# Two rounds of a relational layer and one of a graph convolution summed transposed, with degrees and decoded counts prepared earlier

## The chip, the cores and the metric

The kernel runs on one core of a Trainium2 chip. The metric is the device time of one execution in microseconds. Three executions of the kernel before gave 1709.08, 1710.58 and 1712.69 us; the median is 1710.58 us.

The profile names the engines PE (TensorE, the matrix multiplier; PEld is its loading of the stationary operand), DVE (VectorE), ACT (ScalarE), POOL (GpSimd) and SP (SyncE, which here only issues DMAs). Each works through its own list of instructions in order and waits for the others by semaphores. In a matmul one operand stands still (at most 128 x 128, "stationary") and the other is streamed past it ("moving"); the result lands in PSUM, with the columns of the stationary operand across its partitions and the columns of the moving one along them.

## The reference

Four blocks of a graph network work on 512 nodes with 768 features in float32, over one list of 8704 edges. Each ends with a residual and a layer normalization:

```python
x = _layernorm(x + gat(x))     # layer 0: 8 heads, two rounds
x = _layernorm(x + rgat(x))    # layer 1: 3 edge types, two rounds (r1, r2)
x = _layernorm(x + rgcn(x))    # layer 2: 4 edge types, three rounds (c1, c2, c3)
x = _layernorm(x + gcn(x))     # layer 3: two rounds (d1, d2)
```

The change touches the last two. One round of layer 2 is

```python
out = x @ root + bias
for r in range(4):
    h_r = x @ weight[r]
    # mean over the edges of type r that come into a node
    out = out + segment_sum(h_r[src] * norm[r][:, None], dst)    # norm = 1 / max(degree_r[dst], 1)
```

with a relu behind c1 and c2. One round of layer 3 is `segment_sum((x @ W)[src] * dinv[src] * dinv[dst], dst) + b`, with self loops, where dinv is 1/sqrt of a node's degree, and a relu behind d1.

## The kernel before, in words

**Edges as counts.** The edge list is turned once into matrices of counts: how many edges of a type lead from node s to node t. Seven counts (three types of layer 1, four of layer 2) are packed as digits into one integer; packed_store and packedT_store in DRAM hold that matrix and its transpose. `digit` and `digit_sum` take out a digit or a sum of digits. A sum over edges is then a product with a 512 x 512 matrix cT. Its four tiles of 128 x 512, one per block k of source nodes, have the source nodes across the partitions and the target nodes along them.

**Products in three passes.** A product of 512 nodes x 768 with a weight half (768 x 384) keeps float32 accuracy in three passes[...]. The nodes lie transposed as S: three tiles hi, lo and df of 128 x 6 x 512, six chunks of 128 features across the partitions, 512 nodes along them. The weight half is cut the same way into hm, lo and df (`split_piece`: ACT L771, DVE L772 and L773, three pieces of 128 x 768 per half, loaded by SP at L759 at most three ahead). `product` runs over the four blocks of 128 nodes: six times L814 (hi with hm) and L817 (lo with lo), an ACT instruction that scales the sum in place (L820), and six times L825 (df with df). The six of L825 come behind the next group's twelve (`open_group`, `close_group`), so that PE doesn't wait for ACT. The piece of S (128 features x 128 nodes) is stationary, and the weights move, 384 wide. The result has nodes across and features along.

**A round of layer 2.** Two root products go into acc (`keep`, with the bias added on DVE). Then eight products follow, one for each type r and half j. Each result h is split into hi and lo by `split_h` (ACT L1669, DVE L1670), again with nodes across. After each product comes the aggregation of the one before it, `agg`: for each of four blocks of target nodes eight matmuls (L1682, L1686), with cT's 128 x 128 piece stationary and h moving, 384 wide. DVE multiplies the sum by 1/degree, a number per partition, and adds it to acc in one instruction (L1790).

**Between rounds.** acc has nodes across, but S needs features across. `split_nodes` transposes each block of 128 nodes on PE, two groups of six pieces in halves of three (L785), and cuts the result: hi on ACT with the relu (L790), lo and df on DVE (L792 or L794, L795). `last_two` lets that run between the last aggregations, and the end of block 3 runs inside the next round's first product (`late_end`). d1 passes to d2 in the same way; its aggregation is `agg` at L1841.

**Degrees and counts.** In c1 and half 0 the h tile carries two more columns of ones, so the matmuls of L1682 are 386 wide there, and the extra column of the sum is the degree: L1786 copies it, L1787 and L1788 make 1/degree. The cT tiles are decoded in c1 between the groups of a product: `digit` on DVE (L165), a cast on ACT (L1703). The sum of the digits plus the identity, for layer 3, is made with the last type (L1712). SP stores the tiles to cT_store, and c2, c3 and d1 fetch them from there by POOL's queue, 1 MB each (L1757).

**Before layer 2.** r2, the last round of layer 1, has its three types' products first (r_p), with the first softmax steps among them (L1448, L1451, L1453, L1457). Then `sum2` sums each of four node blocks over 12 pieces of softmax weights (soft_wT, transposed by PE at L1473), in two halves (r_o, L1621), normalizes the block (`norm`, L843 to L849) and hands it to `split_nodes` (x_t).

**Order.** The program is written in one order, and a scheduler orders each engine's instructions by estimated times and dependences, so that an instruction can stand far from where its line is. SP, POOL, ACT and DVE run what it gave them in that order.

Of the kernel before, what the change touches and what calls it, by code (L numbers as in the profile page):

```python
# [8 lines left out]
F32 = mybir.dt.float32  # L9
# [13 lines left out]
P = 128  # L23
# [11 lines left out]
def gnn_stack_kernel(ctx: ExitStack, tc: tile.TileContext, a: dict, out: bass.AP):  # L35
# [125 lines left out]
    flag = const.tile([1, 1], I32, tag="flag", name="flag")  # L161

# [546 lines left out]
    def split_layers():  # L709
# [93 lines left out]
        def product(left, evac, name, between=()):  # L803

            u = used[0]
            used[0] += 1
            while cut[0] < PIECES * (u + 1):
                split_piece()
            hm, lo, df = forms.pop(u)
            for b in range(NB):  # L810
                bs = slice(b * P, (b + 1) * P)
                po = bank(f"{name}_{b}")
                for k in range(KC):
                    nc.tensor.matmul(  # L814
                        po[:, :HD], left[0][:, k, bs], hm[:, k, :], start=(k == 0), stop=False
                    )
                    nc.tensor.matmul(  # L817
                        po[:, :HD], left[1][:, k, bs], lo[:, k, :], start=False, stop=(k == KC - 1)
                    )
                nc.scalar.mul(po[:, :HD], po[:, :HD], SPLIT + 1.0)  # L820
                close_group()

                def rest(b=b, bs=bs, po=po):
                    for k in range(KC):
                        nc.tensor.matmul(  # L825
                            po[:, :HD], left[2][:, k, bs], df[:, k, :],
                            start=False, stop=(k == KC - 1), skip_group_check=True,
                        )
                    evac(b, po)

                open_group.append(rest)
                for job in between[b : b + 1]:
                    job()
                split_piece()
# [92 lines left out]
        with (  # L927
# [107 lines left out]
            seen = g.tile([P, 2, NB], F32, tag="seen", name="seen")  # L1035
# [234 lines left out]

            def check_counts():
# [14 lines left out]
            for i in range(H0):  # L1286
# [7 lines left out]
                elif i + 1 < H0:  # L1294
# [7 lines left out]
                    elif i == 3:  # L1302
                        more = [lambda: None, check_counts]
# [55 lines left out]
        with (  # L1359
# [245 lines left out]

            def finish2(b):
# [4 lines left out]
            def sum2(b, wT):  # L1611
# [3 lines left out]
                for j in range(2):  # L1615
# [14 lines left out]
                    )  # L1630
                    if j == 0 and b:
                        finish2(b - 1)
# [28 lines left out]
        def new_h(name):  # L1661
            hi = work.tile([P, NB, HD + 2], F32R, tag="h_hi", name=f"{name}_hi")
# [3 lines left out]
        def split_h(h, b, po, scale=None):  # L1666
            hi, lo = (t[:, b, :HD] for t in h)
# [9 lines left out]
        def aggregate(cT, h, b, name, ones=0):  # L1677
# [3 lines left out]
            for k in range(NB):  # L1681
                nc.tensor.matmul(  # L1682
                    po[:, : HD + ones], cT[:, k, bs], h[0][:, k, : HD + ones],
                    start=(k == 0), stop=False,
                )
                nc.tensor.matmul(  # L1686
                    po[:, :HD], cT[:, k, bs], h[1][:, k, :], start=False, stop=(k == NB - 1)
                )
            return po

        packedT = tail.tile([P, NB, N], I32, tag="packedT", name="packedT_b")
        nc.sync.dma_start(packedT, packedT_store)
# [4 lines left out]
        def decode(cT, r, k):  # L1697

            v = packedT[:, k, :]
            if r < R4 - 1:  # L1700
                d = work.tile([P, N], I32, tag="dig", name=f"dig{r}_{k}")
                digit(d, v, R3 + r)
                nc.scalar.copy(cT[:, k, :], d)  # L1703
            else:
                sums = [
                    work.tile([P, N], I32, tag=f"dig{i}", name=f"sum{i}_{k}") for i in range(2)
                ]
                for i in range(2):
                    digit_sum(sums[i], v, 3 * i)
                nc.vector.tensor_sub(cT[:, k, :], sums[0], sums[1])  # L1710
                t = work.tile([P, N], F32R, tag="tot", name=f"tot{k}")
                nc.scalar.copy(t, sums[0])  # L1712
                diag = t[:, k * P : (k + 1) * P]
                nc.vector.tensor_add(diag, diag, ident)
                nc.sync.dma_start(cT_store[R4, :, k, :], t.bitcast(F32))
            if k == NB - 1:
                nc.sync.dma_start(cT_store[r], cT.bitcast(F32))

# [3 lines left out]
        deg = tail.tile([P, R4, NB], F32, tag="deg", name="deg")  # L1722
        rdeg = tail.tile([P, R4, NB], F32, tag="rdeg", name="rdeg")
        dinv = tail.tile([P, NB], F32, tag="dinv", name="dinv")

# [19 lines left out]
        late_end = None  # L1745


        for i in (1, 2, 3):
            name = f"c{i}"
            brow = bias_row(a[f"L2_gnn_b{i}"], f"{name}_b")  # L1750
            brows = {i: brow}
            cTs = {}

            def fetch(r):
                cTs[r] = new_c(f"{name}_cT{r}")
                if i > 1:
                    nc.gpsimd.dma_start(cTs[r], cT_store[r])  # L1757

            if i == 3:
                for b in range(NB - 1):  # L1760
                    residual(x_store[1, b], b, brow)
            for j in range(2):

                def keep(b, po, i=i, j=j, brow=brow):
                    half = acc[:, b, columns_of(j)]
                    other = half if i == 3 else brow[:, columns_of(j)]
                    nc.vector.tensor_add(half, po[:, :HD], other)

                jobs = ()
                if late_end:  # L1770

                    def job(late_end=late_end, i=i, brow=brow):
# [149 lines left out]
```

## Time and profile before

| what | us |
|---|---|
| median of three runs | 1710.58 |
| profiled execution | 1706.29 |
| its span, first to last instruction | 1704.70 |
| PE busy | 1619.9 (95%) |
| DVE busy | 1181.0 (69%) |
| ACT busy | 772.3 (45%) |
| POOL busy | 54.0 (3%) |

The granted clock of PE over the whole span is 0.976 of full speed. The stages that matter here, by the times at which they run in the profiled execution:

| stage | from | to |
|---|---|---|
| r2's last product and softmax steps | 994 | 1015 |
| r2's sums (r_o) | 1015 | 1082 |
| c1 | 1085 | 1262 |
| c2 | 1262 | 1438 |
| c3 | 1438 | 1618 |
| d1 | 1618 | 1661 |
| d2 | 1661 | 1704 |

All times below are counted from the start of the span. In a row of the profile the line and engine come first, then the operation, the tile written, the tiles read, and the shapes; "x6" is a number of instructions. In the order of time the first two columns are start and length in us, and "[2.88 <-DVE r_y L849]" is idle time of the engine just before, with what ended it. A PE matmul overlaps the next one, so its pace is the distance of starts, not its length.

### The profile page before, as it was taken

What the parts mean: (1) busy time and instruction counts of PE and PEld (TensorE: products, weight loads), DVE (VectorE), ACT (ScalarE), POOL (GpSimd) and SP (SyncE); (2) the same over time, 40 slices, a digit from 0 to 9 for tenths busy, and PEclk for the clock granted to TensorE, in tenths of its full rate; (3) what the DMA queues carried; (4) which work ended last, traced back from release to release, by engine and by line L of the source; (5) the groups of instructions that cost most, each with busy time, mean ns of one, the idle gap of its engine ahead of it and who ended that gap; (6) DMA issues with size and microseconds to landing.
All of it is one profiled execution on the core that took longest, in us unless ns stands there. A gap on an engine that the chain in (4) does not pass through costs nothing.

```text
span 1704.7 us, 22298 instructions
## 1 busy us (share of the span) xinstructions
PE 1619.9 (95%) x8571; PEld 1444.5 (85%) x8571; DVE 1181.0 (69%) x2185; ACT 772.3 (45%) x1340; POOL 54.0 (3%) x71
## 2 busy tenths in 40 slices
PE   5999999999999999998898899999999999999897
PEld 2868879697887958898898796799999999999897
DVE  8978889786978797545784773655766456654764
ACT  5755656454545544333873371333333333323242
POOL 0000000000000010000001000000000002000001
PEclk8999999999999999998899999999999999999999
DMA  3333323132322222321003241332333224332321
GB/s 122 98 94 103 97 84 124 56 101 76 119 67 83 66 93 75 94 66 56 33 25 134 70 139 37 142 93 81 112 99 107 83 89 143 102 90 81 114 64 54
DMA packets 81266, 151.93 MB, mean 89 GB/s; under 512 B 5768, under 2 KB 67584, under 8 KB 79360
## 3 DMA queue, kind: packets, MB, share of 16 engines
q1 hardware_dynamic: 76048, 125.96, 23.9%
q0 software_dynamic: 3600, 20.47, 3.6%
q10 hardware_dynamic: 1504, 4.00, 0.6%
q8 instruction: 69, 1.13, 0.3%
q14 instruction: 45, 0.37, 0.1%
HBM read 133.63 MB, written 16.78 MB: 88 GB/s over the span
## 4 chain that ended last, share of the span: by engine, by line
PE 81%; DVE 12%; ACT 4%; issue 1%; DMA 1%; ACTq 0%; DVEq 0%; SPq 0%
PE g_o L1117 10%; PE c_p L825 6%; PE c_p L817 6%; PE c_p L814 6%; PE c_a L1682 4%; PE c_a L1686 4%; PE r_o L1621 4%; PE g_p L814 3%; PE g_p L817 3%; PE g_s L817 3%; PE g_s L814 3%; PE g_p L825 3%; PE g_s L825 3%; PE r_p L814 3%; PE r_p L817 3%; PE r_p L825 2%
## 5 line engine op out<-in xcount | busy, mean ns | idle before, releaser
L772 DVE SCALAR_TENSOR_TENSOR w<-w,raw 128x768 fp32r<-128x768 f32 x234 | 221.6, 953 | 120.8 <-ACT w L771 120.0
L771 ACT ACTIVATE w<-raw 128x768 fp32r<-128x768 f32 x234 | 195.1, 839 | 121.0 <-PE c_p L814 34.3
L773 DVE TENSOR_TENSOR w<-w,w 128x768 fp32r<-128x768 f32 x234 | 219.1, 950 | 2.9 <-PE r_p L825 1.5
L817 PE MATMUL c_p<-w,s 128*128 128x384 f32 x576 | 192.5, 334 | 0.0
L814 PE MATMUL c_p<-w,s 128*128 128x384 f32 x576 | 192.5, 334 | 0.0
L1117 PE MATMUL g_o<-wT,g_h 128*128 128x512 f32 x384 | 166.8, 594 | 6.7 <-ACT wT L1073 6.7
L1117 PEld LDWEIGHTS g_o<-wT,g_h 128*128 128x128 f32 x384 | 72.3, 190 | 96.4 <-issue 86.8
L1670 DVE TENSOR_TENSOR c_h_lo<-c_p,c_h_hi 128x384 fp32r<-128x384 f32 x96 | 53.2, 554 | 129.9 <-ACT c_h_hi L1669 129.9
L814 PE MATMUL g_p<-w,s 128*128 128x384 f32 x384 | 134.7, 351 | 0.0
L820 ACT ACTIVATE c_p<-c_p 128x384 f32<-128x384 f32 x96 | 45.6, 475 | 192.9 <-PE c_p L817 192.5
L814 PE MATMUL g_s<-w,y 128*128 128x384 f32 x384 | 132.0, 344 | 0.0
L817 PE MATMUL g_s<-w,y 128*128 128x384 f32 x384 | 130.4, 340 | 1.0 <-DVE y L1135 1.0
L1682 PE MATMUL c_a<-c_h_hi,c_cT 128*128 128x384 f32 (+1 forms) x384 | 130.9, 341 | 0.0
L1686 PE MATMUL c_a<-c_h_lo,c_cT 128*128 128x384 f32 x384 | 130.3, 339 | 0.0
L817 PE MATMUL g_p<-w,s 128*128 128x384 f32 x384 | 129.7, 338 | 0.1
L825 PE MATMUL c_p<-w,s 128*128 128x384 f32 x576 | 117.9, 339 | 0.0
L814 PEld LDWEIGHTS c_p<-w,s 128*128 128x128 f32 x576 | 108.2, 188 | 0.0
L817 PEld LDWEIGHTS c_p<-w,s 128*128 128x128 f32 x576 | 108.1, 188 | 0.0
L825 PEld LDWEIGHTS c_p<-w,s 128*128 128x128 f32 x576 | 100.0, 188 | 5.3 <-ACT c_p L820 5.3
L814 PE MATMUL r_p<-w,s 128*128 128x384 f32 x288 | 100.5, 349 | 0.0
L817 PE MATMUL r_p<-w,s 128*128 128x384 f32 x288 | 98.6, 342 | 0.0
L825 PE MATMUL g_p<-w,s 128*128 128x384 f32 x384 | 79.3, 340 | 0.4 <-ACT g_p L820 0.3
(290 smaller groups left out, 3293.4 us busy)
## 6 DMA issues: line engine op xcount, KB each, us to landing
raw<-in_L_gnn_W_dram SPq DMA_DIRECT2D x222, 384.0 KB
c_cT<-cT_store POOLq DMA_DIRECT2D x8, 1024.0 KB, 5.7
raw<-in_L_gnn_root_dram SPq DMA_DIRECT2D x18, 384.0 KB
r_log<-log_store SPq DMA_DIRECT2D x8, 768.0 KB
cT_store<-c_cT SPq DMA_DIRECT2D x4, 1024.0 KB
g_s<-in_L_gnn_a_src_dram POOLq DMA_DIRECT2D x8, 384.0 KB, 4.2
g_d<-in_L_gnn_a_dst_dram POOLq DMA_DIRECT2D x8, 384.0 KB, 4.4
log_store<-z SPq DMA_DIRECT2D x12, 256.0 KB
```

The lines of the kernel that those rows point to most:

```text
L771: nc.scalar.mul(hm, w, ROUND / SPLIT)
L772: nc.vector.scalar_tensor_tensor(lo, hm, -SPLIT, w, op0=ALU.mult, op1=ALU.add)
L773: nc.vector.tensor_sub(df, hm, lo)
L814: nc.tensor.matmul(po[:, :HD], left[0][:, k, bs], hm[:, k, :], start=(k == 0), stop=False)
L817: nc.tensor.matmul(po[:, :HD], left[1][:, k, bs], lo[:, k, :], start=False, stop=(k == KC - 1))
L820: nc.scalar.mul(po[:, :HD], po[:, :HD], SPLIT + 1.0)
L825: nc.tensor.matmul(po[:, :HD], left[2][:, k, bs], df[:, k, :], start=False, stop=(k == KC - 1), skip_group_check=True,)
L1117: nc.tensor.matmul(po, self.h[k][:, c * P : (c + 1) * P], wT[:, k, :], start=(k == 0), stop=(k == NB - 1),)
L1621: nc.tensor.matmul(po[:, :n], wT[:, k, :], source(k, at), start=(k == 0), stop=(k == NK - 1),)
L1670: nc.vector.tensor_sub(lo, po[:, :HD], hi)
L1682: nc.tensor.matmul(po[:, : HD + ones], cT[:, k, bs], h[0][:, k, : HD + ones], start=(k == 0), stop=False,)
L1686: nc.tensor.matmul(po[:, :HD], cT[:, k, bs], h[1][:, k, :], start=False, stop=(k == NB - 1))
```

## The change

Four edits, made together.

1. c1, c2 and d1 sum transposed. A new `product_columns` makes the root product with the weight piece stationary and S moving, 512 nodes wide, in three groups per half instead of four; `aggregate_columns` does the same for the sums over edges, with h stationary and cT moving. The results have features across and nodes along, as S needs them: `columns_to_S` cuts each chunk of 128 features (hi on ACT, lo and df on DVE), and these rounds have no transposes. The bias becomes a number per partition (ACT). 1/degree is now a row along the nodes: DVE multiplies by it and adds in a second instruction. c3 and d2, and all products with the weights of the types, stay as they were.
2. The degrees are counted in layer 0, beside heads 3 and 4, from the packed counts (`degrees`: per block of 128 nodes three digits and three sums on DVE and a load of 256 KB). Before c1 1/degree and dinv are made of them at once. `row_on_all_of` spreads each of the five onto all partitions, with four PE transposes and a copy on ACT: four times during c1, once before d1. The columns of ones go.
3. The counts are decoded in r2's sums, three of 20 steps per half block, and stored tile by tile (256 KB); c1 fetches its cT from DRAM as the later rounds do.
4. The residual of c3 and d2 is loaded and added for all four blocks at once, instead of three and one.

```diff
-        def product(left, evac, name, between=()):
+        def next_unit():
...
+        def group(out, passes, evac):
+            for k, ((l0, r0), (l1, r1)) in enumerate(zip(passes(0), passes(1))):
+                nc.tensor.matmul(out, l0, r0, start=(k == 0), stop=False)
+                nc.tensor.matmul(out, l1, r1, start=False, stop=(k == KC - 1))
+            nc.scalar.mul(out, out, SPLIT + 1.0)
+            close_group()
...
+        def product_columns(left, j, evac, name, between=()):
+            w = next_unit()
+            for i in range(HK):
+                cs = slice(i * P, (i + 1) * P)
+                po = bank(f"{name}_{i}")
+                group(
+                    po,
+                    lambda f, cs=cs: [(w[f][:, k, cs], left[f][:, k, :]) for k in range(KC)],
+                    lambda i=i, po=po: evac(j * HK + i, po),
+                )
...
+            def degrees(b):
+                v = work.tile([P, N], I32, tag="elu_y", name=f"packed4_{b}")
+                nc.sync.dma_start(v, packed_store[b])
+                for r in range(R4 - 1):
+                    d = work.tile([P, N], I32, tag="elu_e", name=f"d4_{b}_{r}")
+                    digit(d, v, R3 + r)
+                    nc.vector.tensor_reduce(deg[:, r, b : b + 1], d, axis=AX.X, op=ALU.add)
...
+            def decode(k, r):
+                v = spare_int[k % 2]
+                if r == 0:
+                    nc.sync.dma_start(v, packedT_store[:, k, :])
+                t = spare[5 + r % 4]
+                if r < R4 - 1:
+                    d = spare_int[2 + r]
+                    digit(d, v, R3 + r)
+                    nc.scalar.copy(t, d)
...
+                nc.sync.dma_start(cT_store[r, :, k, :], t)
...
+                    for _ in range(3):
+                        if decodes:
+                            decode(*decodes.pop(0))
                     if j == 0 and b:
                         finish2(b - 1)
...
+        def aggregate_columns(cT, h, i, name):
+            po = bank(f"{name}_{i}")
+            cs = slice(i * P, (i + 1) * P)
+            for k in range(NB):
+                for f in range(2):
+                    nc.tensor.matmul(
+                        po, h[f][:, k, cs], cT[:, k, :],
+                        start=(k + f == 0), stop=(k == NB - 1 and f == 1),
+                    )
+            return po
...
+        def row_on_all_of(row, cols, name):
+            po = bank(name)
+            on_all(po, [cols[:, b : b + 1] for b in range(NB)], name)
+            nc.scalar.copy(row, po)
+
+        def columns_to_S(u, c):
+            hi, lo, df = (t[:, c, :] for t in S)
+            nc.scalar.activation(hi, u, AF.Relu, scale=ROUND)
+            nc.vector.scalar_tensor_tensor(lo, u, 0.0, hi, op0=ALU.max, op1=ALU.subtract)
+            nc.vector.scalar_tensor_tensor(df, lo, SPLIT, hi, op0=ALU.mult, op1=ALU.subtract)
...
+            def agg_columns(r, j):
+                for at in range(HK):
+                    c = j * HK + at
+                    po = aggregate_columns(cTs[r], hs[r, j], at, f"{name}_a{r}_{j}")
+                    t = work.tile([P, N], F32, tag="t", name=f"{name}_t{r}_{c}")
+                    nc.vector.tensor_mul(t, po, rdeg_row[:, r, :])
+                    nc.vector.tensor_add(accT[:, c, :], accT[:, c, :], t)
+                    if r == R4 - 1:
+                        columns_to_S(accT[:, c, :], c)
...
+            if i == 1:
+                for c in range(KC):
+                    j, at = divmod(c, HK)
+                    po = aggregate_columns(cT, hs[j], at, f"{name}_a{j}")
+                    t = work.tile([P, N], F32, tag="t", name=f"{name}_t{c}")
+                    nc.vector.tensor_mul(t, po, dinv_row)
+                    nc.scalar.activation(t, t, AF.Relu, bias=bias_column("L3_gnn_b1", c))
+                    columns_to_S(t, c)
+                continue
```

## The prediction

> **What bounds the kernel now.** I read the busy row first, then the busy time of each engine in stretches, then the instructions in order of time where the change touches them.
>
> ```profile
> PE 1619.9 (95%) x8571; PEld 1444.5 (85%) x8571; DVE 1181.0 (69%) x2185; ACT 772.3 (45%) x1340; POOL 54.0 (3%) x71
> ...
> 994.00:1045.00 51.00, 51.00 (x237) 39.19 (x236) 32.94 (x44) 26.61 (x41) 0.78 (x1) 1.00 0.32 109
> 1092.00:1260.00 168.00, 168.00 (x963) 166.15 (x962) 110.11 (x225) 63.75 (x119) 1.07 (x2) 1.00 0.35 111
> 1260.00:1440.00 180.00, 180.00 (x1043) 178.02 (x1042) 106.50 (x164) 61.57 (x118) 7.57 (x9) 1.00 0.33 102
> 1440.00:1603.00 163.00, 163.00 (x931) 161.23 (x930) 91.15 (x133) 54.73 (x101) 5.44 (x6) 1.00 0.31 97
> ```
>
> After each window and its length stand PE, PEld, DVE, ACT and POOL busy, then the granted clock. Layer 2 (1092 to 1603 us) has no hole on PE at full clock, and DVE has 58 us to spare in its first round. There a PE instruction taken away is time won, one added is time lost, and DVE work counts only where PE comes to wait for it.
>
> **Wide matmuls: -0.7 (-3.6 to 0).** Root products (288) and aggregations (576) of c1, c2 and d1 are 384 wide; in their place come 216 + 432 = 648 of 512. PE moves the same columns.
>
> ```profile
> 1189.43 0.33 PE L814 MATMUL c_p<-w,s 128*128 128x384 f32 x1
> ...
> 1191.51 1.20 PE L825 MATMUL c_p<-w,s 128*128 128x384 f32 x6
> ```
>
> Twelve starts lie in 2.08 us: 0.1733 each; thirty aggregation matmuls from 1194.15 to 1199.39 give 0.1747. The only 512-wide matmuls of this type, r_r and gl_r (L914), come in sixes; r_r are six in 1.55 us with the last one 0.394 long: 1.156/5 = 0.231. So 288 x 0.1733 + 576 x 0.1747 = 150.5 against 648 x 0.231 = 149.7. If the part of 0.1733 that isn't streaming (half of the 0.32 that the half clock shows below, 0.160, leaves 0.0133) were fixed per instruction, a wide one would take 0.2133 + 0.0133 and the gain be 3.6; at exactly 4/3 it is 0. I take the measured row.
>
> **Transposes gone: -8.2.** 48 in c1 and c2 and 24 in d1, in twelve sixes.
>
> ```profile
> 1255.56 0.34 PE L1686 MATMUL c_a<-c_h_lo,c_cT 128*128 128x384 f32 x1
> 1255.74 0.82 PE L785 MATMUL c_t<-ident,acc 128*128 128x128 f32 x6
> 1256.32 0.44 PE L1682 MATMUL c_a<-c_h_hi,c_cT 128*128 128x386 f32 x1
> 1256.59 0.35 PE L1686 MATMUL c_a<-c_h_lo,c_cT 128*128 128x384 f32 x1
> ```
>
> From 1255.56 to 1256.59 are 1.03 us, of which two matmuls at the usual pace are 0.35: 0.68 per six, and PE doesn't wait around them. (Three sixes of d1, at 1652, 1655 and 1657 us, cost the same.) 12 x 0.68 = 8.2.
>
> **Rows spread over partitions: +1.8 (+1.5 to +2.2).** Five times four transposes: 1/degree in c1, dinv before d1.
>
> ```profile
> 988.01 1.04 PE L881 MATMUL r_k<-ident,r_cols 128*128 128x128 f32 x8
> 988.80 0.42 PE L814 MATMUL r_p<-w,s 128*128 128x384 f32 x1
> 989.06 0.34 PE L817 MATMUL r_p<-w,s 128*128 128x384 f32 x1
> ```
>
> Eight took 0.79, and the matmul behind them 0.26 for 0.17: 0.88, so 0.44 per four and 1.8 for the four in c1. The four of dinv fall into the gaps of 2.39 and 4.16 us that PE has before d1 (at 1606 and 1617 us), which stay. Without that cover they are 0.4 more.
>
> **Decoding moved to r2: +0.4 (0 to +3).** 36 integer operations on DVE (0.42 each, started every 0.33 to 0.38), 4 subtractions (0.68) and 4 short ones are some 17 us; 16 casts on ACT (0.62) are 10; SP gets 4 loads and 20 stores of 256 KB. In the built order they lie early, between the softmax steps of r2, about 994 to 1045 us. There DVE is busy for 33 of 51 us and ACT for 27: 50 and 37 after the change. It fits, but each step stands in front of something: casts before the scaling by SPLIT + 1 (L820), for which the last six matmuls of a group wait; digits before the softmax of blocks 2 and 3; stores before the load of r_log, on SP. Followed step by step, the last product's scaling comes some 0.35 us late, and block 2's softmax 0.7 to 2 us late where its transposes aren't due before 1031 us. Block 0's normalization ends near 1040.0 instead of 1035.3, PE asks for it at 1040.1. The upper end is a miss there and at one softmax. In c1 the same work leaves DVE, SP and ACT free, which is worth 0: PE never waits for them there. Its cT tiles come back by POOL's queue in 5.7 us and are due a whole product (18 us) later.
>
> **Degrees into layer 0: 0 (0 to +0.6).** Four blocks of 3 digits and 3 sums over 512 (0.68 each), some 3 us each, and four loads on SP. They meet idle stretches of DVE, 5.96 us at 337 and 5.48 at 412, as pairs of 6 to 6.6. What is over delays the weight split behind them, which has a product's time.
>
> **Start of c1: +1.2 (+0.5 to +3).** Now a root group streams all 512 nodes, so its first matmul needs the split of node block 3, where before it needed block 0 alone. And four short operations on DVE (1/degree, dinv; 0.15 each) come into the last block's chain instead of one.
>
> ```profile
> 1079.57 2.74 PE L1621 MATMUL r_o<-xr,soft_wT 128*128 128x384 f32 x8
> 1085.19 1.51 PE L785 MATMUL x_t<-ident,r_y 128*128 128x128 f32 x6 [2.88 <-DVE r_y L849]
> ...
> 1086.83 0.52 PE L817 MATMUL c_root<-w,s 128*128 128x384 f32 x1
> ...
> 1090.99 0.44 PE L814 MATMUL c_root<-w,s 128*128 128x384 f32 x1
> 1091.27 0.34 PE L817 MATMUL c_root<-w,s 128*128 128x384 f32 x1
> ```
>
> 0.45 for the three more operations; then hi on ACT (0.49) and lo on DVE (0.55) of the last half before its matmuls, of which the three root groups taken in turn hide a part: 0.75.
>
> **The three new transitions (c1 to c2, c2 to c3, d1 to d2): +1.2 together (0 to +3.6).** A chunk of 128 columns now needs on DVE a multiply, an add, lo and df (d1: no add), and the next layer's groups need all six chunks. Count from the start of the last aggregation. Its six chunks take PE 48 x 0.231 = 11.1 us; the next layer's groups are taken in turn over chunks 0 to 4, 38 wide matmuls in c2, so chunk 5's lo is due at 19.9 us (c3: 50 narrow ones, 19.8). DVE starts at 1.85, has 23 operations before that lo ends, and three weight splits at 0.87. All depends on their spacing:
>
> ```profile
> 331.57 0.69 DVE L1135 TENSOR_TENSOR y<-g_y,y 128x512 fp32r<-128x512 f32 x1 [0.70 <-ACT y L1134]
> 332.29 0.69 DVE L1136 SCALAR_TENSOR_TENSOR y<-y,y 128x512 fp32r<-128x512 f32 x1
> ...
> 398.30 0.68 DVE L1136 SCALAR_TENSOR_TENSOR y<-y,y 128x512 fp32r<-128x512 f32 x1
> 398.90 0.74 DVE L1130 SCALAR_TENSOR_TENSOR g_y<-g_o,bcols,g_e 128x512 f32<-128x512 f32 x1
> ```
>
> 0.72 where an operation needs the one before it, 0.60 where it doesn't. In the built order neighbours belong to different chunks, so 1.85 + 23 x 0.60 + 2.6 = 18.3: in time. The Trainium skill (VectorE: DVE Perf Modes, "The DRAIN you can't avoid") says that a Vector operation doesn't start before the pipe of the one before is empty; that is 0.69 each, 20.3, and PE waits about 0.4 per transition. At 0.72 it is 21.0 and 1.2. The 0.60 row contradicts the rule, but hops between engines are in neither sum, so I take 0.4. For d1 to d2 the same working gives 16.6 against 16.8.
>
> The residual loads for c3 and d2 now stand together on SP ahead of weight pieces, with four additions of 1.84 us on POOL behind them: done about 29 us after the aggregation's start, the last root group reads them at 30. Cost 0; a miss would only hold DVE.
>
> **Sum:** -0.7 - 8.2 + 1.8 + 0.4 + 0 + 1.2 + 1.2 = -4.3. The profiled execution took 1706.29 (span 1704.70, 1.59 around it), so 1702.0; the median of the runs shown, 1710.58, lies 4.29 above it, so 1706.3.
>
> **Rivals.**
> (1) Instruction overhead is fixed and the transitions are clean: -3.6 - 8.2 + 1.8 + 0.4 + 1.2 = -8.4, 1702.2. For it: half the slow pace is 0.160; against: the r_r row, of six only.
> (2) On the other side: DVE becomes the bound at the transitions, and PE's clock falls. In the rows above PE idles 2.88 us and then runs at 0.32 per matmul until 1091: 13 matmuls lose 1.9, the transposes 0.5. The Trainium skill (TensorE: Matmul & The Clock Gate, "What's actually happening") gives idle windows of about 3.4 us as the cause and as much work to get back; here 2.88 sufficed, so I go by the trace. By either, short stalls cost only themselves, and one of 2.9 costs 2.9 + 2.4 = 5.3. That needs DVE at 22.8 instead of 18.3, a spacing of 0.80. Three times 5.3 in place of 1.2 is +14.7, so 1721; two of the three, 1716. It decides from a mean loss of 3.0 per transition. For it: the chain passes PE, DVE, ACT and DVE again; against: 0.60 in the trace.
> (3) The decoding is late in r2 and eats what the transposes give: +3 there, +3 at the start of c1 and 1.2 elsewhere: -4.3 + 2.6 + 1.8 = +0.1, 1710.7: no change.
>
> **How the numbers follow.** Forecast 0.42, (1) 0.15, (2) 0.23, (3) 0.20. I call 0.2% (3.4 us) what can be told from no change: below 1707.2 is faster, above 1714.0 slower. The forecast's own range is 1703 to 1709: 0.33 faster, 0.09 same. (1) is faster. (2) reaches from 1712 to 1721: 0.20 slower, 0.03 same. (3), 1706 to 1716: 0.04 faster, 0.09 same, 0.07 slower. Together 0.52, 0.21 and 0.27. The range, 1700.5 to 1717, leaves out the upper third of (2) and the low ends.
>
> **What would show it.** Right: no c_t of c1 and c2 and no d_t of d1; 512-wide matmuls every 0.231 us; PE idle under 1 us at each transition, clock 1.00; DVE spacing there near 0.60; the start of c1 about 1.2 us longer between r_o and the full pace; r_o of r2 starting as late after r_p as before. Wrong: PE waits for s by DVE with slow matmuls behind them (2), or waits for x_t, soft_wt or r_p's scaling around 1010 to 1045 (3).

## The result, and the profile after

The changed kernel takes 1703.77 us (median of 15 runs, 1701.15 to 1710.91) against 1710.58 us before (15 runs, 1705.50 to 1719.44). The ratio is 0.9957, with a 95% interval of 0.9941 to 0.9973: faster by 0.4%. The forecast was 1706.3.

The execution that was profiled for the changed kernel is the slowest of its fifteen, 1710.91 us with a span of 1709.1, so its total must not be set against the 1706.29 us profiled before. A second profile of each kernel (the first experiment below) settles what belongs to the change. The busy rows and the head of the chain of work of the changed kernel:

```profile
PE 1614.4 (94%) x8303; PEld 1409.1 (82%) x8303; DVE 1206.2 (71%) x2162; ACT 785.5 (46%) x1353; POOL 55.1 (3%) x72
...
PE 75%; DVE 15%; ACT 5%; DMA 2%; issue 2%; ACTq 0%; DVEq 0%; SPq 0%
```

The next view is the busy time of each engine in the stretches of c1, c2 and c3, with the columns of the prediction's first fence:

```profile
1103.00:1267.00 164.00, 164.00 (x864) 152.10 (x864) 95.30 (x134) 61.53 (x112) 1.59 (x3) 1.00 0.30 91
1267.00:1440.00 173.00, 172.78 (x891) 158.25 (x890) 109.80 (x158) 63.05 (x113) 2.12 (x4) 1.00 0.31 96
1440.00:1610.00 170.00, 167.50 (x953) 164.21 (x951) 103.13 (x148) 57.08 (x106) 11.36 (x9) 1.00 0.33 103
```

PE still fills c1 and c2, with fewer instructions. DVE fell in c1 (110 of 168 us before), and c3 now has 2.5 us in which PE is idle, where it had none. That DVE and POOL are busier in the last window is in part its place: it begins with c3, where the window of before began 4.4 us behind c3's start. From one stage's first matmul to the next one's, in us:

| | c1 | c2 | c3 | d1 | d2 | c1 to the end | c1 starts at |
|---|---|---|---|---|---|---|---|
| before, first profile | 175.5 | 173.7 | 182.8 | 39.9 | 46.5 | 618.4 | 1086.4 |
| before, second profile | 175.5 | 173.7 | 182.8 | 39.9 | 46.5 | 618.4 | 1090.6 |
| changed, first profile | 172.4 | 170.0 | 184.8 | 38.0 | 46.5 | 611.7 | 1097.5 |
| changed, second profile | 170.9 | 170.0 | 185.3 | 37.2 | 46.5 | 609.7 | 1094.2 |

The gain is made where it was forecast: 3.1 to 4.6 us in c1, 3.7 in c2, 1.9 to 2.7 in d1. One stage, c3, lost 2.0 to 2.5. Ahead of c1 both kernels move by several us from execution to execution.

### The profile page after: what moved, and what is told of

Its sections match the earlier page's. It is cut to its first block, busy times and chain, and to the rows that moved or that the text cites. A ratio compares the mean times of both kernels' runs of the same rounds, so it can differ in the third digit from the quotient of the medians.

```text
span 1709.1 us, 21771 instructions
## 1 busy us (share of the span) xinstructions
PE 1614.4 (94%) x8303; PEld 1409.1 (82%) x8303; DVE 1206.2 (71%) x2162; ACT 785.5 (46%) x1353; POOL 55.1 (3%) x72
## 4 chain that ended last, share of the span: by engine, by line
PE 75%; DVE 15%; ACT 5%; DMA 2%; issue 2%; ACTq 0%; DVEq 0%; SPq 0%
PE g_o L1143 10%; PE c_p L825 6%; PE c_p L818 6%; PE c_p L819 6%; PE c_a L1768 5%; PE r_o L1691 4%; PE g_p L818 3%; PE g_p L819 3%; PE g_s L818 3%; PE g_s L819 3%; PE g_s L825 2%; PE c_a L1756 2%; PE g_p L825 2%; PE r_p L818 2%; PE r_p L819 2%; PE r_p L825 2%
## 5 line engine op out<-in xcount | busy, mean ns | idle before, releaser
L818 PE MATMUL g_s<-w,y 128*128 128x384 f32 x384 | 132.3, 345 | 3.2 <-ACT y L1160 3.2
L819 PE MATMUL g_s<-w,y 128*128 128x384 f32 x384 | 130.2, 339 | 1.0 <-DVE y L1161 1.0
L825 PE MATMUL g_s<-w,y 128*128 128x384 f32 x384 | 78.7, 340 | 0.2 <-ACT g_s L820 0.2
L818 PEld LDWEIGHTS g_s<-w,y 128*128 128x128 f32 x384 | 73.1, 190 | 4.2 <-ACT y L1160 4.0
```

What stands on the lines that cost most here:

```text
L818: nc.tensor.matmul(out, l0, r0, start=(k == 0), stop=False)
L819: nc.tensor.matmul(out, l1, r1, start=False, stop=(k == KC - 1))
L825: nc.tensor.matmul(out, l2, r2, start=False, stop=(k == KC - 1), skip_group_check=True)
```

## The experiments

**Is the later start of c1 of the change?** Both kernels were profiled again without an edit.

> The changed kernel as it is, for a second profile. If PE bounds layers 2 and 3 and the start of c1 came 11 us later in the first profile (1097.45 against 1086.36) by chance, then the stages from c1's first root matmul to the end are as before within 0.5 us each (172.4, 170.0, 184.8, 38.0 and 46.5 us), and the start of c1 moves by several us, towards 1087 to 1092, since the run profiled first was the slowest of its fifteen. The rival, that counting degrees in layer 0 and decoding in r2 cost the 11 us, expects c1 to start at 1097 again within 1 us.

> The kernel before, as it is, for a second profile. From c1's first root matmul to the end it took 618.4 us; if the gain is made there, it does so again within 1 us, while the stages ahead of c1 move. In particular, four POOL additions meet the last elu steps of layer 0 (from the first gl_r to the first r_p 59.5 us before, 64.3 to 64.8 in five profiles of the changed kernel and its variants), and r1 (first r_p to the last r_r) took 286.3 against 288.2 to 288.9. If both are chance, they come out between these values now; if they come from the change, they are 59.5 and 286.3 again.

The changed kernel's median was 1705.13 us in ten more runs (ratio to before 0.9967, interval 0.9947 to 0.9987). Its stages from c1 on repeated (table above), and c1 started 3.2 us earlier, less far than I had expected. The kernel before had its second profile in an execution of 1710.53 us. The two stretches that looked like the change's are in it: layer 0's end (first gl_r to first r_p) took 65.3 us, for 59.5 in its first profile and 64.3 and 64.4 in the changed kernel's two; r1 (first r_p to last r_r) took 283.4, for 286.3 before and 288.4 and 288.2 changed. r1 came out at 288.4 in a variant of the kernel before, too, and at 283.4 in one of the changed kernel (both below). So the long stretches occur without the change as well. With it they are the rule: all eight profiles of the changed kernel and its variants that leave layer 0's additions in their place have 64.3 to 64.8 and 288.2 to 288.9. Until the first gl_r, the part in which the degrees are counted, 632.3 and 633.7 us stand against 630.9 to 636.0, mean 632.9, in nine profiles of the changed kernel and its variants. Whether the change costs more ahead of c1 than the 0.4 us found below is therefore not settled: behind c1's start the two profiles gained 6.7 and 8.7 us, the medians of the whole 6.8 and, in the ten runs, 4.9 (1705.13 for 1709.99 beside it).

**What do transposes cost?** Twelve sixes of transposes were put back, of a tile that nothing needs.

```diff
+        def six(c, name):
+            if 1 <= c <= 4:
+                for j in range(2):
+                    pt = bank(f"{name}_x{c}_{j}")
+                    for i in range(HK):
+                        nc.tensor.transpose(
+                            pt[:, i * P : (i + 1) * P], rdeg_row[:, 0, i * P : (i + 1) * P], ident
+                        )
...
                     if r == R4 - 1:
+                        six(c, name)
                         columns_to_S(accT[:, c, :], c)
...
+                    six(c, name)
                     columns_to_S(t, c)
```

> The changed kernel with twelve sixes of transposes on PE added, four in each of c1, c2 and d1 among the last aggregations, of a tile that nothing needs; the results are not read. If a six costs the 0.68 us that the prediction read, c1, c2 and d1 are 2.7 us longer each, 8.2 in all, less what falls into a wait of PE. The rival, that transposes were hidden anyway, expects 0.

It took 1719.06 us in one run; from c1 to the end 621.0. c1 was 173.6 (2.7 more than the second profile of the changed kernel), c2 172.3 (2.3 more), d1 41.4 (3.4 to 4.2 more than in the two profiles). In PE's order of time:

```profile
1259.54 0.39 PE L1768 MATMUL c_a<-c_cT,c_h_lo 128*128 128x512 f32 x1
1259.77 0.82 PE L1807 MATMUL c_x<-ident,rdeg_row 128*128 128x128 f32 x6
1260.34 0.48 PE L1768 MATMUL c_a<-c_cT,c_h_hi 128*128 128x512 f32 x1
1260.65 0.40 PE L1768 MATMUL c_a<-c_cT,c_h_lo 128*128 128x512 f32 x1
```

From 1259.54 to 1260.65 are 1.11 us, less two matmuls at 0.227: 0.66 for a six. The price of the prediction stands, and nothing hides it. c3, where no six was put, also grew, by 2.1 to 2.5 us; that belongs to the question after the next two.

**What does a wide matmul cost?** 504 of the 648 were cut into two of 256 columns.

```diff
-                    nc.tensor.matmul(
-                        po, h[f][:, k, cs], cT[:, k, :],
-                        start=(k + f == 0), stop=(k == NB - 1 and f == 1),
-                    )
+                    for hs in in_two(po, 0 < 2 * k + f < 2 * NB - 1):
+                        nc.tensor.matmul(
+                            po[:, hs], h[f][:, k, cs], cT[:, k, hs],
+                            start=(k + f == 0), stop=(k == NB - 1 and f == 1),
+                        )
```

> The changed kernel with 504 of its 648 wide matmuls cut into two of 256 columns (all but the first and last of each group; same results). If each matmul carries a fixed 0.0133 us above its columns, as 0.1733 for 384 and 0.2267 for 512 say, a half takes 0.1067 + 0.0133 = 0.120 and the kernel is 504 x 0.0133 = 6.7 us longer: some 2.6 in c1 and c2 each, 0.5 in d1, where PE sets the pace. The rival, a cost in proportion to the columns (0.231 for 512, as the prediction took it), expects 0. If the weight load sets the pace of short matmuls, a half takes more than 0.120.

First the changed kernel's aggregation, then this variant's, by PE's order of time (columns: start, length):

```profile
1266.01 0.39 PE L1768 MATMUL c_a<-c_cT,c_h_lo 128*128 128x512 f32 x1
...
1267.60 0.39 PE L1768 MATMUL c_a<-c_cT,c_h_hi 128*128 128x512 f32 x1
```

```profile
1257.99 0.39 PE L1778 MATMUL c_a<-c_cT,c_h_lo 128*128 128x256 f32 x2
...
1259.41 0.40 PE L1778 MATMUL c_a<-c_cT,c_h_lo 128*128 128x512 f32 x1
```

Seven wide ones start in 1.59 us, 0.227 each; twelve halves in 1.42, 0.118 (the median of 480 is 0.119). The kernel before has 0.173 for 384. From 256 to 384 the step is 0.054, from 384 to 512 again 0.054: 0.053 would be 128 columns at 0.4167 ns, half of the 0.32 us that 384 take at half clock divided by 384. What is left over is 0.012 to 0.013 us per matmul at each of the three widths. So the overhead is fixed over these widths. c1 and c2 were 2.8 and 2.7 us longer; each holds 234 of the 504 matmuls that were cut, which makes 0.012 us for one. (The 2.6 that I expected was worked out wrongly: 234 x 0.0133 are 3.1.) d1 was 0.8 to 1.6 longer. The single run took 1714.09 us. Its c3 grew as well.

**How near is DVE to being the bound at the transitions?** Two more multiplications per chunk stand behind lo and df.

```diff
             nc.vector.scalar_tensor_tensor(df, lo, SPLIT, hi, op0=ALU.mult, op1=ALU.subtract)
+            for e in range(2):
+                more = work.tile([P, N], F32, tag="more", name=f"more{c}_{e}")
+                nc.vector.tensor_mul(more, u, rdeg_row[:, 0, :])
```

> The changed kernel with two more multiplications of 128x512 on DVE per chunk behind lo and df at the three transitions (12 each; their result isn't used). By the count of the prediction, chunk 5's lo then ends some 11 x 0.60 = 6.6 us later, at 24.9 us for 19.8 due, so PE waits about 5 us at c1 to c2 and at c2 to c3 and 5 to 7 at d1 to d2, about 15 in all; and since these waits come in pieces under 2 us, the clock should stay at 1.00 for most of them. If instead an idle PE loses its clock here too, it is up to 2.4 us more for each, 22. If the count left much slack out, under 8.

c1, c2 and d1 took 170.9, 169.9 and 37.5 us: nothing more. Only c3 grew, to 188.1. One run took 1707.77 us. At c1 to c2 the last lo came out 25.4 us after the first matmul of the aggregation, as expected, for 20.2 in the changed kernel, but PE's only wait in that stretch was:

```profile
1279.70 2.58 PE L825 MATMUL c_root<-s,w 128*128 128x512 f32 x10 [0.16 <-ACT c_root L820]
```

The misjudged part was mine: the time at which PE needs the last chunk is not fixed. In this variant the scheduler gave PE another order, with more work in front: 59 matmuls of the next layer had started when the last lo ended, for 36 in the changed kernel. Rival (2) of the prediction is refuted up to this load for c1 to c2 and d1 to d2, and my deciding point for it was too near. At c2 to c3 PE waited 2.0 us, for 1.0 and 1.6 in the changed kernel's two profiles; additions on POOL run there too (next experiment), and this run doesn't part the two.

**What stretched c3?** In the changed kernel DVE, POOL and PE show the following between c2 and c3 (first DVE, then POOL, then PE's waits):

```profile
1441.55 0.68 DVE L1870 TENSOR_TENSOR c_t<-c_a,rdeg_row 128x512 f32<-128x512 f32 x1
1442.15 1.75 DVE L1806 SCALAR_TENSOR_TENSOR s<-acc,s 128x512 fp32r<-128x512 f32 x1
1443.83 0.68 DVE L1871 TENSOR_TENSOR acc<-acc,c_t 128x512 f32<-128x512 f32 x1
1444.43 0.68 DVE L1807 SCALAR_TENSOR_TENSOR s<-s,s 128x512 fp32r<-128x512 f32 x1
1445.04 0.68 DVE L1870 TENSOR_TENSOR c_t<-c_a,rdeg_row 128x512 f32<-128x512 f32 x1
1445.63 1.75 DVE L1806 SCALAR_TENSOR_TENSOR s<-acc,s 128x512 fp32r<-128x512 f32 x1
```

```profile
1441.27 2.09 POOL L1815 TENSOR_TENSOR acc<-acc,c_b 128x768 f32<-128x768 f32 x1 [0.43 <-DMA acc<-x_store]
1444.87 1.96 POOL L1815 TENSOR_TENSOR acc<-acc,c_b 128x768 f32<-128x768 f32 x1 [1.52 <-DMA acc<-x_store]
```

```profile
1443.96 0.62 PE L819 MATMUL c_root<-w,s 128*128 128x384 f32 x2 [0.48 <-DVE s L1806]
1447.43 0.79 PE L819 MATMUL c_root<-w,s 128*128 128x384 f32 x3 [0.55 <-DVE s L1806]
```

Beside both additions of the residual that run here on POOL, the DVE operation that reads two tiles of SBUF (L1806) takes 1.75 us instead of 0.68. It ends 0.54 and 0.55 us behind POOL's addition (1443.90 for 1443.36, 1447.38 for 1446.83), so it looks held until POOL is through rather than slowed. The multiplication that reads PSUM and one tile of SBUF (L1870, 1441.55) is not held. The trace of the kernel before has the same meeting, only without a wait of PE behind it, so it could have been read ahead of the change (df operations, which read two tiles of SBUF, alone and beside POOL, then POOL's addition):

```profile
1431.49 1.02 DVE L795 SCALAR_TENSOR_TENSOR s<-s,s 128x384 fp32r<-128x384 f32 x2
1434.92 1.83 DVE L795 SCALAR_TENSOR_TENSOR s<-s,s 128x384 fp32r<-128x384 f32 x2
```

```profile
1434.03 1.84 POOL L1732 TENSOR_TENSOR acc<-acc,c_b 128x768 f32<-128x768 f32 x1 [23.21 <-DMA acc<-x_store]
```

In the changed kernel it happens before d1, too (DVE, POOL, PE):

```profile
1619.70 2.07 DVE L777 TENSOR_TENSOR w<-w,w 128x768 fp32r<-128x768 f32 x1
1621.70 0.15 DVE L875 RECIPROCAL l_rstd<-l_rstd 128x1 f32<-128x1 f32 x1
```

```profile
1619.17 1.79 POOL L1815 TENSOR_TENSOR acc<-acc,d_b 128x768 f32<-128x768 f32 x1 [29.43 <-DMA acc<-x_store]
```

```profile
1622.62 1.54 PE L789 MATMUL c_t<-ident,acc 128*128 128x128 f32 x6 [5.17 <-DVE acc L876]
1623.95 1.06 PE L908 MATMUL dinv<-ident,dinv 128*128 128x128 f32 x4
1624.67 0.67 PE L818 MATMUL d_p<-w,s 128*128 128x384 f32 x1
```

PE at the same place in the kernel before:

```profile
1617.17 1.54 PE L785 MATMUL c_t<-ident,acc 128*128 128x128 f32 x6 [4.16 <-DVE acc L849]
1618.37 0.67 PE L814 MATMUL d_p<-w,s 128*128 128x384 f32 x1
```

There a weight split that nobody is in a hurry for (0.95 elsewhere) stands in front of the normalization of c3's last blocks, and PE waits 5.17 us for it, for 4.16 before the change. The four transposes of dinv's row do not lie in this wait but behind it: from c_t to d1's first matmul are 2.05 us, for 1.20 before. The Trainium skill (GPSIMD Engine Reference, "1. Specifications") says that POOL shares its SBUF interfaces with DVE, and that DVE operations with two inputs in SBUF, or in a two-port mode, contend. The operations that stretch here fit that. Two variants test it. One leaves POOL's additions of bias to the residual out, with the loads in place. The other moves them: c3's bias goes into DVE's addition of the root product and its residual is added on POOL during the first product of the types; d2's bias row is made to depend on the last chunk of S, so that POOL can't add it until d1 has handed over.

```diff
             nc.sync.dma_start(acc[:, b, :], x_of)
-            nc.gpsimd.tensor_tensor(acc[:, b, :], acc[:, b, :], brow, op=ALU.add)
```

> The additions of bias to the residual on POOL are left out for c3 and d2 (the biases of these two rounds are not added; everything else is kept). If two lo operations took 1.75 us instead of 0.68 at c2 to c3, and a weight split 2.07 instead of 0.95 at c3 to d1, because POOL was adding at the same time, then all of these go back to 0.68 and 0.95, PE waits 0 instead of 1.0 us for S at c2 to c3, and 4.1 instead of 5.2 us for acc before d1: c3 is 182.4 to 182.9 instead of 184.8 us, the whole some 2.1 us shorter. The rival, that DVE's own order makes these waits, expects 184.8 and the same long operations.

```diff
-                    nc.vector.tensor_add(half, half, po[:, :HD])
+                    nc.vector.tensor_add(half, po[:, :HD], brow[:, columns_of(j)])
...
+                if i == 3 and at == 0:
+                    for b in range(NB):
+                        xr = work.tile([P, D], F32, tag="xres", name=f"xres{b}")
+                        nc.sync.dma_start(xr, x_store[1, b])
+                        nc.gpsimd.tensor_tensor(acc[:, b, :], acc[:, b, :], xr, op=ALU.add)
...
+        def late(brow):
+            z = tail.tile([P, 1], F32, tag="late", name="late_z")
+            ends = S[2][:, KC - 1, N - 1 :].bitcast(F32)
+            nc.gpsimd.tensor_tensor(z, ends, ends, op=ALU.subtract)
+            nc.gpsimd.tensor_tensor(brow[:, 0:1], brow[:, 0:1], z, op=ALU.add)
...
-                for b in range(NB):
-                    residual(x_store[2, b], b, brow)
+                late(brow)
+                for b in range(NB):
+                    nc.gpsimd.tensor_tensor(acc[:, b, :], acc[:, b, :], brow, op=ALU.add)
```

> The same additions on POOL, complete, but not at the transitions: c3's residual is added during its first products, d2's bias after d1 has handed over S (d2's residual is still in acc and isn't loaded again). If only the meeting with the transitions costs, this gives the same 2 us as leaving the additions out (c3 at 182.4 to 182.9 us), and DVE's weight splits, which then meet POOL instead, are long but hidden. The rival: long weight splits come back to PE later, and c3 and d2 together gain nothing.

| | c1 | c2 | c3 | d1 | c1 to the end | median us, ratio to before |
|---|---|---|---|---|---|---|
| additions left out | 170.8 | 170.0 | 182.0 | 38.6 | 607.8 | 1699.40, 0.9920 (0.9889 to 0.9951) |
| additions later | 170.8 | 170.0 | 182.0 | 38.5 | 607.6 | 1703.04, 0.9961 (0.9947 to 0.9976) |
| later, and layer 0's too (below) | 170.9 | 170.0 | 182.8 | 38.3 | 608.3 | 1697.07, 0.9926 (0.9906 to 0.9945) |

With the additions moved, DVE at the same place is even, and PE has no wait there:

```profile
1441.79 0.68 DVE L1806 SCALAR_TENSOR_TENSOR s<-acc,s 128x512 fp32r<-128x512 f32 x1
1442.38 0.68 DVE L1875 TENSOR_TENSOR acc<-acc,c_t 128x512 f32<-128x512 f32 x1
1442.99 0.68 DVE L1807 SCALAR_TENSOR_TENSOR s<-s,s 128x512 fp32r<-128x512 f32 x1
```

c3 is 182.0 us in the first two, 2.8 to 3.3 less than in the changed kernel. With the additions left out, DVE runs the same operations in the same order as in the changed kernel at both places, without the long ones (the weight split before d1 takes 0.91 us instead of 2.07), so DVE's order isn't the cause. In the first profile of the changed kernel the meetings cost 1.7 us at c2 to c3 and 1.1 before d1. In the second they cost 2.3 and 0.2; the other 0.8 is PE's clock, at half from 1607.4 to 1610.8 behind an earlier wait of 2.39 us. The kernel before (1606.6 to 1610.0) and the third line of the table (1593.2 to 1596.7) have this too, the first two lines have not. So the residual additions cost 2.5 to 2.8 us by where they ran, not by being late.

The same explains most of the growth of c3 in three other variants: in each POOL met the last normalization (one step of it took 1.97 us instead of 0.68), and PE waited there 6.9 (sixes), 6.7 (more DVE work) and 6.9 us (halves), for 5.2 and 4.2 in the changed kernel. The rest is at c2 to c3, where PE waited 2.1, 2.0 and 1.8 us.

d1 is 0.5 to 1.4 us longer in the first two variants than in the changed kernel, with 3.8 us of it at half clock for 2.6 and 0.8. By the medians the moved version is 0.7 below 1703.77 and 2.1 below the 1705.13 of the changed kernel's runs beside it; the intervals overlap, so the gain of c3 is shown by the stages and not by the whole.

**The decoding put back into c1.** The third of the four edits alone was undone.

```diff
-                    for _ in range(3):
-                        if decodes:
-                            decode(*decodes.pop(0))
...
+                        jobs = [
+                            lambda to=to, k=k: decode(cTs[to], to, k) for k in range(NB - 1)
+                        ] + [
+                            lambda to=to: (
+                                decode(cTs[to], to, NB - 1),
+                                row_on_all_of(
+                                    rdeg_row[:, to, :], rdeg[:, to, :], f"rdeg{to}"
+                                ),
                             )
                         ]
```

> The counts are decoded in c1 again, as before the change; the transposed sums and the degrees in layer 0 stay. PE-bound: r2 from its last product to the end of r_o loses the 0.3 us that decoding cost there, c1 keeps its 172.4 us within 1 us, because DVE would be busy some 114 of 164 us; the whole is -0.5 to +1. The first rival: decoding in r2 was what made c1 start late, so -5 or more. The second: with the transposed sums DVE can't carry the decoding in c1 any more, so c1 is 3 us or more longer.

It took 1705.48 us (10 runs; 0.9960, 0.9943 to 0.9976), not to be told from the changed kernel. From the last r_r to the end of r_o it needed 104.14 us, exactly as before the change (104.15 and 104.14), while eight profiles with the decoding in r2 have 104.4 to 104.8. c1 was 173.0 us, of which 2.3 were lost to a slow clock at its start; DVE is busy for 109 of 164 us in it, 95 in the changed kernel. Both rivals fall: the decoding is not what made c1 start 11 us late, and DVE could have carried it in c1. Moving it costs 0.4 us in r2 and brings nothing in the course of c1. At c1's start there is more to it. PE busy, its granted clock, DMA share and GB/s in the kernel before, in this variant and in the second profile of the changed kernel:

```profile
1084.40:1091.20 6.80, 6.00 (x21) 0.50 0.63 243
```

```profile
1091.00:1097.80 6.80, 5.96 (x17) 0.50 0.67 241
```

```profile
1090.00:1104.00 14.00, 10.85 (x50) 1.00 0.58 207
```

In all four profiles without the decoding in r2 (two of the kernel before, one of its variant below, and this one) the clock is at half for 6.8 us, from some 2.1 us after the beginning of PE's idle 2.9. Of the eight with it in r2, seven have no half clock there and one has 3.4 us. So the slow start of c1 goes with where the decoding is, and moving it saved some 2 us there in most profiles. Why the clock then holds is open. The 0.2 to 0.6 us by which r2 is longer may shift the wait against the clock's steps, but no run tests that.

**The same meeting at the end of layer 0.** Four additions on POOL also run there, in both kernels. In the second profile of the changed kernel, POOL and then DVE:

```profile
632.41 8.25 POOL L1364 TENSOR_TENSOR xin<-xin,gl_b 128x768 f32<-128x768 f32 x4 [44.30 <-DMA xin<-in_x_dram]
```

```profile
632.98 1.80 DVE L1161 TENSOR_TENSOR y<-g_y,y 128x512 fp32r<-128x512 f32 x1 [0.99 <-ACT y L1160]
634.71 2.06 DVE L1154 TENSOR_SCALAR g_e<-g_e 128x512 f32<-128x512 f32 x1
636.69 2.30 DVE L1162 SCALAR_TENSOR_TENSOR y<-y,y 128x512 fp32r<-128x512 f32 x1
638.91 0.74 DVE L1156 SCALAR_TENSOR_TENSOR g_y<-g_o,bcols,g_e 128x512 f32<-128x512 f32 x1
```

These steps of the elu are what PE waits for (3.2 us for L1160's result, behind them). The version that combines both moves, and the kernel before with this one alone:

```diff
                     xin = []
+                    z0 = small.tile([P, 1], F32, tag="late", name="late_x")
+                    ends = Y[2][:, KC - 1, N - 1 :].bitcast(F32)
+                    nc.gpsimd.tensor_tensor(z0, ends, ends, op=ALU.subtract)
+                    nc.gpsimd.tensor_tensor(brow[:, 0:1], brow[:, 0:1], z0, op=ALU.add)
```

> The variant with the later additions of c3 and d2, and with the additions of layer 0's residual on POOL held back until the last elu chunk is cut. If the same meeting of POOL and DVE costs there, DVE's operations between 630 and 640 us go from 1.7 to 2.3 us back to 0.4 to 0.7, and the stretch from the first gl_r to the first r_p goes from 64.3 to 58 or less; with the 2 us at c3 the whole is some 7 to 8 us faster than the changed kernel, near 1696. The rival, that the later additions are then missing at layer 0's last sums, expects PE to wait for xin there and no gain.

> The kernel before, with only the additions of layer 0's residual on POOL held back until the last elu chunk is cut. If the meeting of POOL and DVE there is independent of the change, the stretch from the first gl_r to the first r_p goes from 59.5 and 65.3 us (two profiles) to 58.4, as in the variant of the changed kernel, and the median of the runs falls by some 4 to 6 us, to about 1705. The rival, that this gain needs the changed order, expects no change.

In the combined version, DVE and then POOL:

```profile
632.94 0.69 DVE L1161 TENSOR_TENSOR y<-g_y,y 128x512 fp32r<-128x512 f32 x1 [1.01 <-ACT y L1160]
633.55 0.42 DVE L1154 TENSOR_SCALAR g_e<-g_e 128x512 f32<-128x512 f32 x1
633.89 0.68 DVE L1162 SCALAR_TENSOR_TENSOR y<-y,y 128x512 fp32r<-128x512 f32 x1
```

```profile
637.43 0.19 POOL L1363 TENSOR_TENSOR late_x<-y 128x1 f32<-128x1 f32 x1 [49.65 <-DVE y L1162]
637.70 0.19 POOL L1364 TENSOR_TENSOR gl_b<-gl_b,late_x 128x1 f32<-128x1 f32 x1
637.97 7.21 POOL L1368 TENSOR_TENSOR xin<-xin,gl_b 128x768 f32<-128x768 f32 x4
```

The stretch from gl_r to r_p is 58.4 us, and the kernel takes 1697.07 us (6 runs, 1693.56 to 1702.33; 0.9926 of before, 0.9906 to 0.9945): the fastest here. (Its profiled execution also has the short r1, 283.4 us, which no experiment explains.) The kernel before with only this move takes 1706.41 us (10 runs; 0.9974, 0.9957 to 0.9991), with the stretch at 58.6. So this gain, 4.0 us by the medians, does not need the change.

## Why the prediction was right, and where it was not

The forecast, 1706.3, lies 2.5 us above the measured median; the time is in the range, the direction holds, and the mechanism (PE-bound stages lose transposes) is shown. That it came so near is in part luck, since misses in both directions cancel; rival (1), at 1702.2, was nearer, with its fixed overhead shown and its clean transitions true of two in three. By steps:

| step | forecast | measured |
|---|---|---|
| wide matmuls | -0.7 (-3.6 to 0) | -2.8 |
| transposes gone | -8.2 | -7.9 to -8.2 (12 x 0.66 to 0.68) |
| rows spread | +1.8 | +1.8 (0.44 each in c1), and 0.85 for dinv's before d1 |
| decoding in r2 | +0.4 | +0.4 (104.5 for 104.15) |
| degrees | 0 | nothing beyond the spread of executions |
| start of c1 | +1.2 | -0.6 and -2.2 |
| three transitions | +1.2 | 0.2, 1.7 to 2.3, 0 |
| c3 to d1, residual | 0 | +1.0 and +0.1 |

Without r2's 0.4 the measured steps sum to -5.9 and -7.8 us for the two profiles, in which c1 to the end gained 6.7 and 8.7. The rest is not assigned; the shares of half clock around d1, which differ between profiles, are part of it.

*Wide matmuls* was the largest term mis-sized. I took 0.231 from six matmuls with a stationary operand of two columns; matmuls of the kind that the change makes start every 0.227 us, on the mean every 0.2273 in the root groups and 0.2283 in the aggregations. 216 x 0.2273 + 432 x 0.2283 = 147.7, for 288 x 0.1735 + 576 x 0.1746 = 150.5 in the kernel before. The other bound of that step, the fixed overhead, was the right one, and rival (1) had it.

*Start of c1* was wrong in sign. Between r_o's end and the first root matmul lie 4.00 us, for 4.05 before: the four small operations took gaps of DVE that its chain had anyway (two of them start 0.07 us apart), and the three root groups taken in turn began on hi alone. What differs is the slow clock behind the wait: it cost the first forty root matmuls 2.3 us in both profiles of the kernel before, 1.7 and 0.1 in those of the changed kernel, and 2.3 with the decoding back in c1. The idle time in front is the same 2.9 us in all of them, and I took the loss behind it as given. Over all twelve profiles it is 2.3 in the four without the decoding in r2 and 0.1 in seven of the eight with it, so it is not chance alone, and the forecast for moving the decoding left out what it may do here.

*Rows spread* took dinv's four transposes to fall into PE's gaps before d1. They came behind the last gap, at half clock, and cost 0.85.

*The transitions* were right in two of three. Where no POOL addition runs, DVE keeps the 0.60 spacing that the trace of before had shown (the rows at 1442 us of the version with later additions). The section of the Trainium skill from which the prediction took 0.69 (VectorE: DVE Perf Modes, "The DRAIN you can't avoid") adds that an operation that isn't held starts earlier, which the prediction left out; starts 0.60 apart for operations of 0.68 agree with that. The last lo ends 20.2 us after the aggregation's first matmul, of which 1.4 are six other matmuls that stand behind that first one: 18.8, for 18.3 forecast.

*The step that failed* is the one on the residual: "Cost 0; a miss would only hold DVE". I asked whether the four additions on POOL are done in time. They are; but they ran at the same time as the DVE chain that PE was waiting for and stretched it. With this in c2 to c3 (the groups of the last chunk 1.7 and 2.3 us later than in the variants) and before d1 (1.1 and 0.2) it cost 2.8 and 2.5 us in c3. Wide matmuls gave 2.1 more than forecast and the start of c1 1.8 to 3.4, so the sum came out near all the same.

Single executions of one kernel lie up to 14 us apart (1705.50 to 1719.44 before), and c1's start moves by several us, which is why neither profiled execution stands for its median. By the profiles, c1 to the end gained 6.7 and 8.7 us; by the medians the whole gained 6.8.

Rival (3), late decoding, did not come about, nor did rival (2), DVE as the bound, with the load that the change brings.

## What to carry to other kernels

Where PE sets the pace, count its instructions and price each kind at the step between starts in matmuls of the same shape, the stationary operand's included; a wider moving operand saves the fixed part of each matmul that goes. Check not only whether POOL's elementwise work is in time, but which DVE operations run beside it: put it where DVE's two-input operations have slack, by a dependence if the scheduler would start it as soon as it can. And a due time worked out from one instruction order is no threshold if a scheduler makes the order.

## What the runs showed of the hardware that was not expected

- A POOL addition of two 128x768 tiles (1.8 us alone) makes a DVE operation on 128x512 that starts beside it take 1.75 to 2.30 us instead of 0.68 if it has two SBUF inputs, and an SBUF to SBUF operation with one input 2.06 instead of 0.42. In the rows at c2 to c3 the DVE operation ends some 0.54 us behind POOL's. One with a PSUM input isn't stretched (0.68 at 1441.55, 0.74 at 638.91). POOL's addition is longer too, 1.9 to 2.7 us in the changed kernel's two profiles.
- A matmul of this type starts every 0.119, 0.173 and 0.227 us at 256, 384 and 512 columns: the columns and a fixed 0.012 to 0.013 us.
- The same 2.9 us of idle PE was followed by 6.8 us of half clock in four profiles, 3.4 in one and none in seven: losses of 2.3, 1.7 and 0.1 us. They go with the place of the decoding ahead of it.
